# A two-layer block on one core: short-lived tiles share rings, the token and unit rings grow, and the order is drawn anew

## The chip, the cores and the metric

The kernel runs on one core of a Trainium2 chip. A core has five engines with a queue of their own each: TensorE (PE, matrix products; PEld is its loading of weights), VectorE (DVE), ScalarE (ACT), GpSimd (POOL) and SyncE (SP, which here only issues DMAs). Each engine works through its instructions in the order in which the program put them, and they meet through semaphores. The metric is the device time of one execution in microseconds. Before the change it is 3841.9 us, the median of three executions (3837.64 to 3845.13).

## The reference, cut to what matters

The input x is 32 images of 56 x 56 positions (tokens) with 128 channels. Two layers follow each other, and in each of them a "conv" part and an "ffn" part is added to x.

```python
x = x + L0_conv(ln_c(x))      # batch norm over all tokens, signs, a 3x3 convolution with signs as weights
t = t + L0_ffn(ln_t(t))       # softmax over 8 experts, the best 2 per token, each expert a 128x128 matrix
x = x + L1_conv(ln_c(x))      # per image and per 16 channels: a = sigmoid(p1*p2), b likewise,
                              #   z = einsum('bikc,bkjc->bijc', a, b); gate * (ln(z) @ Wz + bz)
t = t + L1_ffn(ln_t(t))       # 64 experts; each takes its best 8 tokens of every image, pools them,
                              #   two layers with gelu, and adds its output to those 8 tokens
```

The batch norm needs the mean and the variance of all 32 images before the first convolution can be compared with its limit. The product z of L1_conv needs a whole image, and so does the choice of 8 tokens of L1_ffn.

## The kernel before

**Tiling.** A unit is 896 tokens, seven rows of 128 with 128 channels: 3584 bytes in each partition. Two images make a pair of seven units; there are 16 pairs and 112 units.

**Stages.** A first pass (`fetch1`, `stats1`, `norm1`) reads all units, normalises them, turns them by TensorE, stores them and gathers the batch norm's sums. `load_weights` prepares weights meanwhile. `batch_norm` closes it. Then each pair goes through these stages: `fetch` loads a unit's x, `sign` compares the stored values with the limit, `conv` and `conv_back` do the convolution and add it; `moe_stats`, `moe_turn`, `moe_route`, `moe_gates` choose two of eight experts for each token, `moe_experts` multiplies (VectorE scales the turned tokens by the gates in L823, TensorE does eight products in L828), `moe_add` adds. `tri_stats` and `tri_turn` prepare the product of L1_conv. Then comes a chain with little width, called the triangle below: `tri_b` and `tri_a` each make two products per half (L886), ScalarE writes them to `lines` (L899), TensorE turns those (`tr_b`, `tr_a`, by the helper at L473), ScalarE and VectorE multiply the two parts (L914, L919), ScalarE takes the sigmoids (L933 for b, L945 for a); `tri_z` does the product (L972), normalises, and takes z through DRAM into `zc` (L1051). `tri_out` uses it unit by unit and adds to x. `gate_stats`, `gate_turn`, `gate_logits`, `top8` (the best 8 of 3136 tokens on VectorE, and an exponential over all of them on ScalarE, L1211 and L1214) and `pool_rows` do the pair's part of L1_ffn. At the end `late_experts` runs the 64 experts in 16 groups of four for all pairs at once, six groups a second time for the last pair alone, and GpSimd adds their outputs to the tokens in DRAM by 128 indirect DMAs (L1497), two chains of 64 in which each waits until the one before it has landed. `last_sums` and `last_out_rows` finish the last pair.

**What sets the order.** No engine's order is written by hand. Every operation is put into the class `Order` with its engine, an assumed duration in ns, and what it reads and writes. Its rank is a tick: `p * PERIOD + TICK[stage][i]`, with a period of 14 ticks a pair (L1917 to L1923). `Order.run` (L164) then plays the work through in the kernel's own build: at each moment each free engine takes the ready operation of lowest rank whose tiles can be had, for as long as the assumed duration says. The order in which operations are taken is the order in which they are written into the engines' queues. The chip then runs this order with its own durations. Assumed durations and ticks thus change nothing of what is computed, only what stands behind what in each queue.

**Tiles and rings.** A tile is taken from a ring of equal buffers named by a tag (L426 to L431). Before: 12 token tiles "x" and 5 unit tiles "u" of 3584 bytes, 4 "xT" and 3 "yl" of that size, 5 "gb" of 4096 bytes for gates, and small rings of their own for tiles that live briefly: "st1", "q1", "rm1" in the first pass, "rT" in `moe_route`, "abm" (2), "b", "zT" in the triangle, "pt" in `pool_rows`. A pair holds seven "x" tiles from `fetch` to the store in `gate_turn` (L1131). The late experts take "x" tiles too, five a group (L1330, L1379).

Of the kernel before, what the change touches and what calls it, by code (L numbers as in the profile page):

```python
# [25 lines left out]
H = 56  # L26
# [12 lines left out]
    "fetch": (1.14, 2.61, 2.37, -0.16, 7.91, 9.69, 13.32),  # L39
    "sign": (0.38, 0.8, 0.81, 5.7, 6.62, 8.09, 11.62),  # L40
    "conv": (2.4, 3.69, 6.8, 7.72, 10.43, 11.89, 12.86),
    "conv_back": (2.88, 4.08, 7.34, 7.86, 10.43, 11.92, 14.91),
    "moe_turn": (4.53, 5.17, 9.52, 8.55, 12.68, 12.47, 15.14),
    "moe_gates": (6.43, 7.52, 9.89, 10.15, 13.98, 12.85, 16.56),
    "moe_experts": (7.18, 7.67, 10.31, 10.83, 14.93, 12.94, 16.8),
    "moe_add0": (10.78, 13.85, 13.48, 12.98, 18.39, 17.9, 18.29),
    "moe_add1": (10.06, 12.78, 13.45, 11.14, 15.45, 13.84, 17.8),
    "tri_turn": (15.73, 17.37, 18.31, 18.26, 19.34, 19.61, 19.71),
    "moe_stats": (4.26, 8.17, 12.25, 14.94),
    "moe_route": (5.48, 9.71, 12.84, 15.88),  # L50
    "tri_stats": (14.82, 13.52, 18.41, 19.02),
    "tri_b": (19.79, 19.99),
    "tri_a": (19.82, 21.57),
    "tri_z": (21.72,),
    "tri_out": (22.38, 23.42, 24.57, 25.03, 26.33, 28.33, 30.18),
    "gate_stats": (23.97, 24.69, 27.63, 30.31),
    "gate_turn": (25.8, 26.15, 26.94, 28.19, 29.43, 32.04, 32.1),
    "gate_logits": (25.91, 27.01, 28.84, 29.87, 31.66, 33.33, 32.83, 33.54),
    "clear": (31.73,),
    "top8": (34.46,),  # L60
    "pool_rows": (37.33,),
    "late_first": (37.82, 37.92, 38.25, 41.79, 42.31, 42.85),
    "late_alone": (51.08, 41.11, 38.24, 41.73, 42.93, 41.08),
    "late_rest": (39.41, 40.01, 40.1, 40.59, 42.76, 44.26, 47.21, 48.79, 50.74, 58.57),
    "last_sums": (49.02,),
    "last_rows": (63.85,),
# [4 lines left out]
NX, NY = 12, 5  # L71
# [212 lines left out]
def kernel(ctx: ExitStack, tc: tile.TileContext, a: dict, out: bass.AP):  # L284
# [118 lines left out]
    with ExitStack() as c2:  # L403
# [19 lines left out]
        for t in lines:  # L423
# [3 lines left out]
            "x": NX, "u": NY, "ps": 8, "gb": 5, "xT": 4, "yl": 3, "st1": 2, "q1": 2, "rm1": 2,  # L427
# [256 lines left out]
        def moe_route(p, m):  # L684
# [82 lines left out]
            @op("ACT", 210, r=[d], w=[(d, 1)])  # L767
            def _():
                nc.scalar.activation(d.ap[:, 1, :], d.ap[:, 0, :], AF.Sigmoid)
                nc.scalar.activation(d.ap[:, 2, :], d.ap[:, 0, :], AF.Sigmoid, scale=-1.0)  # L770
# [1252 lines left out]
```

## Time and profile before

| | us |
|---|---|
| median of three executions | 3841.9 (3837.64 to 3845.13) |
| the profiled execution | 3851.35 |
| its span, first to last instruction | 3849.5 |
| TensorE busy in the span | 3495.7 |
| VectorE busy | 3149.1 |
| ScalarE busy | 2355.4 |
| GpSimd busy | 407.0 |
| mean granted clock of TensorE | 0.958 |
| from the first pair's product z (L972) to the last pair's, 15 periods | 548.49 to 3476.28 |

The profile gives for each engine its busy time, for each line its instructions and mean duration, and for each idle stretch what ended it ("<-"). The chain of work that ended last goes back from the last instruction to whatever released each step. A table by stretch gives, for windows of the span, each engine's busy time and count of instructions, and TensorE's granted clock (1.00 is full speed). Products in f32 show as two records each. The execution has three parts: the first pass up to about 345 us, the pairs with one period after the other up to about 3500 us, and the additions to the tokens from 3501.23 to 3844.7 us.

### The profile page before, as it was taken

Reading aid. Unit: us, or ns where it says so; the run is one execution under the profiler, and the core shown is the slowest. Engines: PE = TensorE matmul, PEld = TensorE weight load, DVE = VectorE, ACT = ScalarE, POOL = GpSimd, SP = SyncE. Lnnn points to the kernel's source line nnn. Section 1 sums busy time; section 2 is a strip of 40 time slices with the busy share of each in tenths; the row PEclk is TensorE's granted clock in tenths of the full one; section 3 lists DMA queues with packets and bytes.
Section 4 is the critical chain, followed back from the end, with each engine's and each line's share of the span. In section 5 each row is a group of like instructions: output and inputs, shape, how many; then the busy total and the mean of one; then the engine's idle time right before and its main releaser. Section 6 shows DMA issues by size and latency. Waiting matters only on the chain.

```text
span 3849.5 us, 77967 instructions
## 1 busy us (share of the span) xinstructions
PE 3495.7 (91%) x27661; PEld 2836.7 (74%) x27661; DVE 3149.1 (82%) x10452; ACT 2355.4 (61%) x5458; POOL 407.0 (11%) x472
## 2 busy tenths in 40 slices
PE   7999999999999999999999999999999999997653
PEld 6886787777777777778787868686878787865442
DVE  7997879898989898989898989898989898875310
ACT  5997437566666666675757575757575747566210
POOL 1000000100000000000000000101010101003667
PEclk9999999999999999999999999999999999998776
DMA  7997556465656565656565656565656565656774
GB/s 252 349 342 257 199 176 243 174 235 183 230 183 229 176 225 186 224 190 220 191 224 188 219 182 223 188 230 189 230 189 218 201 217 203 203 195 187 211 199 73
DMA packets 325544, 811.90 MB, mean 211 GB/s; under 512 B 86170, under 2 KB 110659, under 8 KB 325155
## 3 DMA queue, kind: packets, MB, share of 16 engines
q1 hardware_dynamic: 262034, 680.39, 51.4%
q10 hardware_dynamic: 41104, 109.20, 7.3%
q0 software_dynamic: 22016, 17.32, 3.1%
q8 instruction: 220, 3.60, 0.4%
q14 instruction: 170, 1.38, 0.1%
HBM read 630.19 MB, written 176.55 MB: 210 GB/s over the span
## 4 chain that ended last, share of the span: by engine, by line
PE 39%; DVE 33%; ACT 11%; DMA 9%; issue 4%; POOL 3%; ACTq 0%; another core or an unknown queue 0%; SPq 0%; DVEq 0%; POOLq 0%
PE acc L828 22%; DVE stln L484 8%; DVE gb L823 7%; DMA gb<-gate 4%; DVE sg L1098 3%; PE ps_cv L629 3%; DMA out<-eo_False,picked 3%; PE gram L1673 3%; POOL out L1497 2%; PE tr L473 2%; DVE x L1107 2%; DVE x L571 2%; ACT ym L558 1%; ACT yt L558 1%; PE ps_z L972 1%
## 5 line engine op out<-in xcount | busy, mean ns | idle before, releaser
L828 PE MATMUL acc<-expert_w,gb 128*128 128x128 f32 x12544 | 1443.9, 276 | 25.2 <-DVE gb L823 13.5
L828 PEld LDWEIGHTS acc<-expert_w,gb 128*128 128x128 f32 x12544 | 1415.1, 192 | 67.3 <-DVE gb L823 33.9
L823 DVE TENSOR_TENSOR gb<-gb,xT 128x1024 f32<-128x1024 f32 x784 | 949.4, 1217 | 64.5 <-DMA gb<-gate 61.5
L484 DVE BATCH_NORM_STATS2 stln<-x 128x6 f32<-128x128 f32 x2352 | 576.4, 281 | 1.9
L558 ACT ACTIVATE ym<-x,rmln 128x128 f32<-128x128 f32 x784 | 322.4, 486 | 244.4 <-DVE rmln L546 243.6
L629 PE MATMUL ps_cv<-frame,w_sign 128*128 128x448 bf16 x2016 | 427.5, 362 | 8.4 <-DVE frame L607 8.4
L558 ACT ACTIVATE yt<-x,rmln 128x128 f32<-128x128 f32 x784 | 324.5, 486 | 123.2 <-DVE rmln L546 120.0
L558 ACT ACTIVATE yl<-x,rmln 128x128 f32<-128x128 f32 x784 | 318.6, 487 | 125.9 <-DVE rmln L543 113.3
L629 PEld LDWEIGHTS <-w_sign 128*128 128x128 bf16 x2016 | 196.4, 99 | 188.5 <-issue 23.8
L1229 POOL DMA_INDIRECT rows<-y,near x128 | 122.2, 955 | 1113.5 <-DVE mk L730 1007.0
L1114 POOL MEMSET a_bd<- 128x2048 f32 x16 | 29.5, 1841 | 1846.3 <-PE ps_zo L1085 1400.7
L840 DVE TENSOR_TENSOR x<-acc,x 128x512 f32<-128x512 f32 x224 | 137.9, 616 | 95.7 <-PE acc L828 95.6
L1497 POOL DMA_INDIRECT out<-eo_False,picked x128 | 197.1, 1540 | 139.0 <-DMA out<-eo_False,picked 74.8
L558 ACT ACTIVATE y<-x,rm 128x128 f32<-128x128 f32 x448 | 194.7, 486 | 20.2 <-DVE rm L543 11.3
L637 ACT ACTIVATE cv<-ps_cv,cv_shift,cv_scale 128x448 f32<-128x448 f32 x224 | 157.9, 725 | 74.8 <-PE ps_cv L629 74.3
L1063 PEld LDWEIGHTS ps_g<-wg,yT 128*128 128x128 f32 x1568 | 187.7, 193 | 21.6 <-issue 15.1
L1063 PE MATMUL ps_g<-wg,yT 128*128 128x128 f32 x1568 | 203.5, 280 | 0.0
L484 DVE BATCH_NORM_STATS2 st<-x 128x6 f32<-128x128 f32 x784 | 179.6, 278 | 24.5 <-DMA x<-in_x 24.2
L1673 PE MATMUL gram<-y 128*128 128x128 f32 x1568 | 196.7, 278 | 0.0
L1673 PEld LDWEIGHTS gram<-y 128*128 128x128 f32 x1568 | 192.3, 198 | 0.0
L579 ACT COPY xT<-trm 128x512 f32<-128x512 f32 x224 | 108.6, 528 | 98.9 <-PE trm L473 79.4
L473 PE MATMUL tr<-ident,y 128*128 128x128 f32 x784 | 139.2, 295 | 29.1 <-ACT y L558 23.1
(244 smaller groups left out, 5295.0 us busy)
## 6 DMA issues: line engine op xcount, KB each, us to landing
gb<-gate SPq DMA_DIRECT2D x784, 512.0 KB
x<-in_x SPq DMA_DIRECT2D x224, 448.0 KB
y<-yT SPq DMA_DIRECT2D x112, 448.0 KB
ys<-y SPq DMA_DIRECT2D x112, 448.0 KB
out<-x ACTq DMA_DIRECT2D x112, 448.0 KB
y<-yl ACTq DMA_DIRECT2D x112, 448.0 KB
w_False<-in_L_ffn_weight SPq DMA_DIRECT2D x128, 256.0 KB
w_True<-in_L_ffn_weight SPq DMA_DIRECT2D x48, 256.0 KB
```

The source lines that it names most:

```text
L473: nc.tensor.transpose(ps.ap[:, n * 128 : (n + 1) * 128], get()[:, n0 + n, :], ident)
L484: nc.vector.bn_stats(st.ap[:, c0 + k, :], src.ap[:, k, :])
L558: nc.scalar.activation(dst.ap[:, k, :], src.ap[:, k, :], AF.Identity, bias=m, scale=r)
L629: nc.tensor.matmul(acc, lhsT=w_sign[:, tap, :], rhs=frames[f][:, 8 * band + kh : 8 * band + kh + 8, kw : kw + W], start=(tap == 0), stop=( ...
L637: nc.scalar.activation(cv.ap[:, :, 64 * h : 64 * h + 64], ps.ap[:, :448].rearrange("c (q n) -> c n q", n=N7), AF.Identity, bias=cv_shift, ...
L823: nc.vector.tensor_tensor(gb.ap, gb.ap, over(xT.ap[:, n, :], E0), ALU.mult)
L828: nc.tensor.matmul(acc.ap[:, n % 4 * C : (n % 4 + 1) * C], lhsT=gb.ap[:, e, :], rhs=expert_w[:, e * C : (e + 1) * C], start=(e == 0), stop ...
L840: nc.vector.tensor_tensor(dst, acc.ap[:, : k * C], dst, ALU.add)
L1063: nc.tensor.matmul(psg.ap[:, n * C : (n + 1) * C], lhsT=yT[:, n0 + n, 16 * u : 16 * u + 16, :].rearrange("c r v -> c (r v)"), rhs=wg, star ...
L1229: nc.gpsimd.indirect_dma_start(out=rows.ap[:, j, :], out_offset=None, in_=y3_d[p], in_offset=bass.IndirectOffsetOnAxis(ap=near.ap[:, k + j ...
L1497: ins = nc.gpsimd.indirect_dma_start(out=tokens_out, out_offset=bass.IndirectOffsetOnAxis(ap=picked[lot][:rows, e : e + 1], axis=0), in_=e ...
L1673: nc.tensor.matmul(gram.ap[:, :C], lhsT=y.ap[:, n, :], rhs=y.ap[:, n, :], start=(g % G16 == 0 and n == 0), stop=(g % G16 == G16 - 1 and n ...
```

## The change

Ten rings of short-lived tiles go or shrink, and their tiles are taken from larger rings. In the first pass "st1" moves into "yl", and "q1" and "rm1" into "xT". "rT" moves into "u". "abm" (two buffers), "b" and "zT" move into "yl". "pt" moves into "pacc". "lg", "k1" and "k2" keep one buffer in place of two. This frees 16,960 bytes of each partition: 1344 + 448 + 448 (first pass), 2048 (rT), 3 x 448 (lg, k1, k2), 4096 (abm), 3584 (b), 3136 (zT), 512 (pt). Three more "x" and one more "u" tile take 14,336.

Six assumed durations on ScalarE are raised: the gates' sigmoids from 210 to 430 ns, those of b from 540 to 960 and 780, those of a from 1000 to 1800 (two instructions), each copy to `zc` from 750 to 1650, and the exponential of `top8` from 2700 to 4300.

All ticks are new. The instructions that are run, their number and their operands stay as they were, but for the buffers that they name.

```diff
 TICK = {
-    "fetch": (1.14, 2.61, 2.37, -0.16, 7.91, 9.69, 13.32),
+    "fetch": (-3.74, -10, -3.13, -14.5, -7.83, 3.11, 10.08),
...
-    "conv": (2.4, 3.69, 6.8, 7.72, 10.43, 11.89, 12.86),
+    "conv": (1.55, 3.6, 7.13, 8.23, 10.33, 11.24, 12.47),
...
-    "moe_experts": (7.18, 7.67, 10.31, 10.83, 14.93, 12.94, 16.8),
+    "moe_experts": (9.97, 8.74, 10.4, 10.31, 14.58, 13.75, 18.16),
...
-    "tri_b": (19.79, 19.99),
-    "tri_a": (19.82, 21.57),
-    "tri_z": (21.72,),
-    "tri_out": (22.38, 23.42, 24.57, 25.03, 26.33, 28.33, 30.18),
+    "tri_b": (19.94, 20.51),
+    "tri_a": (20.49, 22.18),
+    "tri_z": (22.21,),
+    "tri_out": (22.65, 22.27, 24.57, 24.46, 25.73, 26.61, 29.54),
...
-    "gate_logits": (25.91, 27.01, 28.84, 29.87, 31.66, 33.33, 32.83, 33.54),
-    "clear": (31.73,),
-    "top8": (34.46,),
-    "pool_rows": (37.33,),
-    "late_first": (37.82, 37.92, 38.25, 41.79, 42.31, 42.85),
-    "late_alone": (51.08, 41.11, 38.24, 41.73, 42.93, 41.08),
-    "late_rest": (39.41, 40.01, 40.1, 40.59, 42.76, 44.26, 47.21, 48.79, 50.74, 58.57),
-    "last_sums": (49.02,),
-    "last_rows": (63.85,),
+    "gate_logits": (25.65, 27.25, 29.32, 29.3, 30.74, 32.14, 33.59, 34.2),
+    "clear": (29.96,),
+    "top8": (34.73,),
+    "pool_rows": (37.11,),
+    "late_first": (37.25, 38.05, 39.03, 42.4, 43.15, 50.78),
+    "late_alone": (72, 45.56, 46.46, 53.51, 72.6, 48.13),
+    "late_rest": (39.44, 41.8, 46.7, 48.82, 51.44, 55.75, 55.79, 59.9, 61.33, 63.15),
+    "last_sums": (43.28,),
+    "last_rows": (77.43,),
 }
...
-NX, NY = 12, 5
+NX, NY = 15, 6
...
         op = Order({
-            "x": NX, "u": NY, "ps": 8, "gb": 5, "xT": 4, "yl": 3, "st1": 2, "q1": 2, "rm1": 2,
-            "st": 3, "q": 3, "rT": 1, "lg": 2, "k1": 2, "k2": 2, "mk": 2, "d": 2,
-            "gg": 2, "gT": 2, "rm": 4, "abm": 2, "b": 1, "zq": 1, "zT": 1, "lgT": 1,
-            "m8": 2, "i8": 2, "sq": 2, "pg": 2, "near": 2, "pacc": 1, "ptc": 1, "pt": 1,
+            "x": NX, "u": NY, "ps": 8, "gb": 5, "xT": 4, "yl": 3,
+            "st": 3, "q": 3, "lg": 1, "k1": 1, "k2": 1, "mk": 2, "d": 2,
+            "gg": 2, "gT": 2, "rm": 4, "zq": 1, "lgT": 1,
+            "m8": 2, "i8": 2, "sq": 2, "pg": 2, "near": 2, "pacc": 1, "ptc": 1,
         })
...
-            rT = new("rT", [128, 512], f"rT_{name}")
+            rT = new("u", [128, 512], f"rT_{name}")
...
-            @op("ACT", 210, r=[d], w=[(d, 1)])
+            @op("ACT", 430, r=[d], w=[(d, 1)])
...
-            u = new("abm", [128, NV, 4, CH], f"abm_{name}")
+            u = new("yl", [128, NV, 4, CH], f"abm_{name}")
...
-                live[p]["b"] = new("b", [128, CH, W], f"b_s_{p}")
+                live[p]["b"] = new("yl", [128, CH, W], f"b_s_{p}")
...
-            @op("ACT", 540, r=[(u, 0), (u, 4)], w=[(b_s, h)])
+            @op("ACT", (960, 780)[h], r=[(u, 0), (u, 4)], w=[(b_s, h)])
...
-            @op("ACT", 2 * 500, r=[(u, 0), (u, 4)], w=[("a_bd", h)])
+            @op("ACT", 2 * 900, r=[(u, 0), (u, 4)], w=[("a_bd", h)])
...
-            zT = new("zT", [128, N7, 2, H], f"zT_{p}")
+            zT = new("yl", [128, N7, 2, H], f"zT_{p}")
...
-                @op("ACT", 750, r=[(zv, rg) for rg in range(4)],
+                @op("ACT", 1650, r=[(zv, rg) for rg in range(4)],
...
-            @op("ACT", 2700, r=[q, m8], w=all_lg + [(q, 1), (pg, 1)])
+            @op("ACT", 4300, r=[q, m8], w=all_lg + [(q, 1), (pg, 1)])
...
-            pk = new("pt", [2 * K1, 2 * E1], f"pt_{p}")
+            pk = new("pacc", [2 * K1, 2 * E1], f"pk_{p}")
...
-            st = new("st1", [128, G4 * N7, 6], f"st1_{k}")
+            st = new("yl", [128, G4 * N7, 6], f"st1_{k}")
...
-            rm = first["rm", k] = new("rm1", [128, 2, G4 * N7], f"rm1_{k}")
+            rm = first["rm", k] = new("xT", [128, 2, G4 * N7], f"rm1_{k}")
...
-                0.0, "q1",
+                0.0, "xT",
```

More of the change, by code (lines that the diff above doesn't have):

```diff
@@ L38 @@
 TICK = {
-    "fetch": (1.14, 2.61, 2.37, -0.16, 7.91, 9.69, 13.32),
-    "sign": (0.38, 0.8, 0.81, 5.7, 6.62, 8.09, 11.62),
-    "conv": (2.4, 3.69, 6.8, 7.72, 10.43, 11.89, 12.86),
-    "conv_back": (2.88, 4.08, 7.34, 7.86, 10.43, 11.92, 14.91),
-    "moe_turn": (4.53, 5.17, 9.52, 8.55, 12.68, 12.47, 15.14),
-    "moe_gates": (6.43, 7.52, 9.89, 10.15, 13.98, 12.85, 16.56),
-    "moe_experts": (7.18, 7.67, 10.31, 10.83, 14.93, 12.94, 16.8),
-    "moe_add0": (10.78, 13.85, 13.48, 12.98, 18.39, 17.9, 18.29),
@@ L47 @@
[L47 to L51, printed above, removed]
-    "tri_b": (19.79, 19.99),
-    "tri_a": (19.82, 21.57),
-    "tri_z": (21.72,),
-    "tri_out": (22.38, 23.42, 24.57, 25.03, 26.33, 28.33, 30.18),
-    "gate_stats": (23.97, 24.69, 27.63, 30.31),
-    "gate_turn": (25.8, 26.15, 26.94, 28.19, 29.43, 32.04, 32.1),
@@ L58 @@
-    "gate_logits": (25.91, 27.01, 28.84, 29.87, 31.66, 33.33, 32.83, 33.54),
-    "clear": (31.73,),
-    "top8": (34.46,),
-    "pool_rows": (37.33,),
-    "late_first": (37.82, 37.92, 38.25, 41.79, 42.31, 42.85),
-    "late_alone": (51.08, 41.11, 38.24, 41.73, 42.93, 41.08),
-    "late_rest": (39.41, 40.01, 40.1, 40.59, 42.76, 44.26, 47.21, 48.79, 50.74, 58.57),
-    "last_sums": (49.02,),
-    "last_rows": (63.85,),
+    "fetch": (-3.74, -10, -3.13, -14.5, -7.83, 3.11, 10.08),
+    "sign": (-0.46, 0.58, 0.99, 5.76, 7.43, 9.35, 7.45),
@@ new lines @@
+    "conv": (1.55, 3.6, 7.13, 8.23, 10.33, 11.24, 12.47),
+    "conv_back": (3.49, 4.12, 7.45, 8.99, 10.33, 11.5, 14.37),
+    "moe_turn": (4.64, 5.02, 9.64, 9.61, 12.11, 12.05, 15.86),
+    "moe_gates": (7.34, 7.19, 9.81, 10.29, 13.07, 12.37, 17.81),
+    "moe_experts": (9.97, 8.74, 10.4, 10.31, 14.58, 13.75, 18.16),
+    "moe_add0": (12.93, 12.5, 11.9, 14.5, 16.21, 16.41, 18.99),
+    "moe_add1": (13.44, 10.15, 13.46, 11.4, 14.97, 14.28, 18.83),
+    "tri_turn": (17.2, 17.23, 18.18, 18.85, 18.85, 19.68, 19.73),
@@ new lines @@
+    "moe_stats": (4.59, 9.39, 11.74, 14.89),
+    "moe_route": (5.55, 9.69, 12.24, 16.09),
+    "tri_stats": (15.5, 14.58, 18.73, 19.51),
+    "tri_b": (19.94, 20.51),
+    "tri_a": (20.49, 22.18),
+    "tri_z": (22.21,),
+    "tri_out": (22.65, 22.27, 24.57, 24.46, 25.73, 26.61, 29.54),
+    "gate_stats": (23.28, 25.16, 26.82, 30.79),
+    "gate_turn": (24.56, 25.82, 26.81, 27.98, 30.07, 32.08, 31.98),
+    "gate_logits": (25.65, 27.25, 29.32, 29.3, 30.74, 32.14, 33.59, 34.2),
+    "clear": (29.96,),
```

## The prediction

> **What bounds the kernel now.** I read the page's busy times first. No engine is full over the span:
>
> ```profile
> PE 3495.7 (91%) x27661; PEld 2836.7 (74%) x27661; DVE 3149.1 (82%) x10452; ACT 2355.4 (61%) x5458; POOL 407.0 (11%) x472
> ```
>
> Such a share mixes stages, so next comes the table by stretch: thirteen whole periods, then the neighbourhood of one triangle in steps of 5 us (window: length, then busy us of PE, PEld, DVE, ACT, POOL, granted clock, DMA share, GB/s).
>
> ```profile
> 743.00:3286.00 2543.00, 2415.89 (x19650) 1972.11 (x19650) 2264.88 (x7133) 1632.28 (x3639) 142.67 (x130) 0.99 0.59 207
> 1105.00:1110.00 5.00, 5.00 (x37) 3.06 (x39) 4.86 (x15) 4.97 (x10) 1.90 (x2) 1.00 0.06 15
> 1110.00:1115.00 5.00, 2.76 (x34) 0.92 (x23) 3.25 (x17) 4.70 (x6) 3.78 (x4) 1.00 0.20 52
> 1115.00:1120.00 5.00, 2.99 (x20) 1.09 (x18) 3.76 (x6) 2.04 (x6) 3.50 (x3) 1.00 0.14 39
> 1120.00:1125.00 5.00, 4.07 (x20) 2.38 (x21) 2.60 (x9) 4.26 (x10) 0.00 (x0) 0.50 0.05 15
> 1125.00:1130.00 5.00, 5.00 (x36) 3.50 (x36) 2.69 (x9) 4.66 (x11) 0.00 (x0) 0.82 0.00 0
> ```
>
> A period is 2543 / 13 = 195.6 us. TensorE is busy 185.8 of it and VectorE 174.2, so TensorE bounds the period and idles 9.8. The rows show where: from 1110 to 1125 it misses 2.24 + 2.01 + 0.93 us, and then works at half clock. The clock costs 4.07 x 0.5 + 5 x 0.18 = 2.9 us. The waits of TensorE in the same thirteen periods agree (total us, times, longest):
>
> ```profile
> PE tr_a L473 <- ACT lines L899: 40.6, 24, 2.3
> PE tr_b L473 <- issue: 38.4, 13, 3.7
> PE acc L828 <- DVE gb L823: 12.1, 41, 0.8
> ```
>
> The first two are (40.6 + 38.4) / 13 = 6.1 us a period, both for the transposes of `lines`. With the clock the triangle loses 9.0 us in each period; all else together 3.7. ScalarE's instructions in time order say why `lines` is late:
>
> ```profile
> 1108.14 1.28 ACT L1211 ACT_TABLE_LOAD   x1
> 1109.44 0.30 ACT L1211 ACTIVATE pg<-m,sq 128x8 f32<-128x8 f32 x1
> 1109.64 2.90 ACT L1214 ACTIVATE lgT<-lgT,sq 128x3136 f32<-128x3136 f32 x1
> 1112.45 0.18 ACT L1214 ACTIVATION_READ_ACCUMULATOR lgT<-lgT,sq 128x1 f32 x1
> 1112.54 0.71 ACT L637 ACTIVATE cv<-ps_cv,cv_shift,cv_scale 128x448 f32<-128x448 f32 x1
> 1113.15 0.62 ACT L899 ACTIVATE lines<-ps_b,bb 128x448 f32<-128x448 f32 x1
> ```
>
> The exponential of `top8` holds ScalarE from 1108.14 to 1112.6, 4.5 us, where the plan assumes 2.7. The products for b were done by 1111; their copy to `lines` stands behind it, and TensorE's queue behind that copy. Groups by line give the other assumed durations:
>
> ```profile
> L945 ACT ACTIVATE a_bd<-abm_a 56x448 f32<-56x448 f32 x64 | 63.9, 999 | 19.8 <-DVE acc L1249 10.4 <-DVE abm_a L919 9.0
> L1051 ACT COPY a_bd<-zv 128x896 f32<-128x896 f32 x32 | 55.1, 1774 | 5.5 <-DMA zv<-z 5.5
> L933 ACT ACTIVATE b_s<-abm_b 128x512 f32<-128x512 f32 (+1 forms) x32 | 31.6, 988 | 0.0
> ```
>
> Against assumptions of 500, 750 and 540. In the end part the 128 additions bound the time: 343.5 us from 3501.2 to 3844.7, of which these waits are part:
>
> ```profile
> POOL out L1497 <- DMA out<-eo_False,picked: 74.8, 47, 4.6
> ```
>
> [...]
>
> **The change part by part.** *Assumed durations.* Between the products for b and the product z, per pair: the exponential was short by 4.5 - 2.7 = 1.8 us, b by 2 x 0.99 - 1.08 = 0.9, a by 4 x 1.0 - 2.0 = 2.0, together 4.7. The new figures cover 1.6 + 0.66 + 1.6 = 3.9 of it. The old plan so believed the triangle 4.7 us shorter than it is, and left about that much too little other work in TensorE's queue between its transposes; the chip shows 6.1 us idle. A plan that knows of 3.9 can put 3.9 us of convolutions, turns and experts there. I take the idle time as falling from 6.1 to 2.2, and [...] half of the clock's 2.9 comes back: 3.9 + 1.4 = 5.3 us. Work put there must be ready, and some will be missed elsewhere: I take 5.0 a period. VectorE then stands at 174.2 / 190.6 = 91%, still below TensorE. Over 15 periods: 75 us. The `zc` copies (short by 2.05) and the gates' sigmoids (0.84) lie beside experts' products (TensorE is at 5.00 of 5 us after 1135): nothing, and up to 0.5 us a period if that cover is thin.
>
> *Three more "x" tiles.* No instruction is added. SP's own waits in two periods show the ring in use:
>
> ```profile
> SPq L592 <- ACT yl L558: 57.7, 14, 11.6
> ```
>
> SP stands 29 us a period before x loads, with gate loads (L817) queued behind. Yet TensorE's wait through VectorE's gates is 12.1 / 13 = 0.9 us a period, since five "gb" buffers of 8 x 0.223 = 1.8 us each cover 9 us (the chain in order of time runs 448 records in 50.03 us, two to a product). So the ring alone is worth 0 to 0.9; its use is to give the triangle work from the next pair, which I counted above.
>
> *Tiles that move.* "yl": the last `ylT` is read at 1098.5, the first abm copy runs at 1119, z leaves at 1159, the next `ylT` is written at 1188: 20 and 29 us free on the two sides, cost 0. If they met, ScalarE's abm copy would stand before the last `ps_l`, with the copies to `lines` behind it and TensorE's transposes behind those, us for us. "u" holds `rT` for a copy and four transposes, 0.59 + 0.66 us, four times a pair, and has one buffer more: 0. "lg", "k1", "k2" with one buffer serialise batches that stand 60, 57 and 20 us apart (first copies near 1107, 1167, 1224, 1244); 0, or up to a batch's chain of 4 us if two come together. `pk` in "pacc" lives from 1129 to 1134.4, its ring is next wanted a period later: 0. First pass: "yl" and "xT" have no other user but `mean_w`.
>
> *First pass.* From 60 to 100 us, where the weights' four tiles sit in a ring of 5 "u", TensorE is busy 35.09 of 40 at clock 0.83: some 11 us lost. A sixth "u" doubles what is left for the units; I take 4. At the turn to the pairs (340 to 360: 11.62 of 20) earlier x loads may give 2. Bounds 0 and 15.
>
> *End.* The ticks of the late experts are reordered, with the same 128 additions. At best half of the 74.8 us of waits goes (-37); a worse interleaving of the two chains costs as much (+37). I take 0.
>
> Sum on the profiled execution: 3851.4 - 75 - 6 = 3770. It stands 9.4 above the median, so 3761 against 3841.9.
>
> **The rivals.** *The stall goes wholly* (chance 0.15): all 9.0 us x 15 = 135, and the first pass 6: 3701. For it: the expert products are plenty (392 x 0.223 = 88 us a pair). Against: the new ticks still put `tri_b` (19.94) and `tri_z` (22.21) before the next pair's first experts (8.74 + 14 = 22.74), so only ready convolutions, turns and leftover experts are there.
>
> *The change doesn't do what it says* (0.17): the stall is one of data, not of order; each transpose waits for its copy and the filler is not ready. Then only the first pass gains: 3836. For it: 6 us of the wait is "issue" and short pieces. Against: VectorE and ScalarE idle in it as well, so it is order, not load.
>
> *Slower: x loads at the head of SP's queue* (0.16). The new fetch ticks (-14.5 to 10.1) make SP take an x load as soon as the plan sees a buffer free, and the buffer comes free after a store and a normalisation on ScalarE that the chip may end later. SP waits in order, and gate loads stand behind. It decides once a wait outlasts the 9 us that the "gb" ring covers; the longest now is 12.1. Seven loads a pair, each 1.5 us beyond the cover, cost 10 us, less the gain of 5: +5 x 15 = 75, thus 3917.
>
> **How the numbers follow.** The likeliest case, a partly filled triangle, has 0.52 and 3761 (own range 3725 to 3805 with the end's bound). The range 3700 to 3850 leaves out about 0.07 below and 0.13 above. A measurement of this kernel tells 0.2%, some 8 us, from no change. Faster by more than that: 0.51 + 0.15 + 0.10 of the second rival = 0.76; within it 0.08; slower 0.16.
>
> **What would show it.** Right: the distance of z products falls from 195.2 to about 190; the two waits of TensorE for `lines` fall below 3 us a period and the clock's dip in the triangle shrinks; VectorE's waits for gates stay near 61.5 / 16 = 4 us a pair; the additions still take about 343 us. Wrong: the dip unchanged at an unchanged period, x loads at SP with longer waits followed by VectorE idling for gates, or a `tri_b` or `tr_b` waiting for a "yl" reader. The sum fails if the gain sits in the first pass or the end.

## The result, and the profile after

The changed kernel takes 3820.7 us (median of five executions, 3802.54 to 3828.05) against 3842.0 of the kernel before (median of five, 3837.64 to 3848.67). The ratio of the means is 0.9933, with a 95% interval of 0.9905 to 0.9961; all ratios below are of means too. The change makes the kernel faster, by 21 us where 81 were forecast.

The page of the changed kernel, busy time of each engine, and below it the table by stretch: first the same thirteen periods, then one triangle and what follows it (window: length, then busy us of PE, PEld, DVE, ACT, POOL, granted clock, DMA share, GB/s).

```profile
PE 3486.8 (91%) x27661; PEld 2840.6 (74%) x27661; DVE 3154.8 (83%) x10452; ACT 2359.6 (62%) x5456; POOL 409.4 (11%) x472
```

```profile
743.00:3286.00 2543.00, 2433.09 (x19753) 1993.44 (x19751) 2276.47 (x7152) 1643.78 (x3643) 145.09 (x130) 0.99 0.60 208
1290.00:1295.00 5.00, 5.00 (x48) 2.22 (x41) 2.59 (x8) 4.85 (x5) 2.00 (x3) 1.00 0.05 13
1295.00:1300.00 5.00, 3.09 (x29) 2.07 (x26) 3.05 (x10) 4.97 (x12) 3.87 (x4) 1.00 0.23 57
1300.00:1305.00 5.00, 3.33 (x23) 1.09 (x19) 4.72 (x19) 4.94 (x12) 3.50 (x3) 1.00 0.15 39
1305.00:1310.00 5.00, 4.44 (x30) 3.13 (x31) 2.81 (x11) 4.77 (x11) 0.00 (x0) 1.00 0.19 23
1320.00:1325.00 5.00, 5.00 (x33) 5.00 (x33) 5.00 (x8) 1.49 (x4) 0.00 (x0) 0.70 0.20 57
```

In the same 2543 us TensorE is busy 17.2 us more than before (2433.1 against 2415.9), 1.3 us a period. The triangle still has its hole: from 1295 to 1310 TensorE misses 1.91 + 1.67 + 0.56 = 4.1 us. In this period the half clock is no longer inside it but behind the product z, which starts at 1310.8 (the row 1320 to 1325). ScalarE is now full throughout the triangle (4.85, 4.97, 4.94, 4.77 of 5). TensorE's waits in the thirteen periods (total us, times, longest):

```profile
PE tr_a L473 <- ACT lines L899: 35.1, 26, 1.9
PE acc L828 <- DVE gb L823: 19.0, 31, 2.5
PE trm L473 <- ACT ym L558: 15.3, 39, 0.5
PE acc L828 <- DVE rmln L543: 9.5, 11, 0.9
PE tr_b L473 <- ACT lines L899: 1.4, 1, 1.4
```

The wait at `tr_b` is nearly gone (3.0 us a period before, 0.1 now), that at `tr_a` is 2.7 us where it was 3.1. The two together fell from 6.1 to 2.8. The rest of the list is new or larger: gates 0.9 to 1.5 us, `trm` 1.2, `rmln` 0.7. ScalarE in order of time shows what became of the exponential:

```profile
1289.97 1.39 ACT L899 ACTIVATE lines<-ps_b,bb 128x448 f32<-128x448 f32 x2 [0.19 <-PE ps_b L886]
1291.38 1.28 ACT L1211 ACT_TABLE_LOAD   x1
1292.67 0.30 ACT L1211 ACTIVATE pg<-m,sq 128x8 f32<-128x8 f32 x1
1292.88 2.89 ACT L1214 ACTIVATE lgT<-lgT,sq 128x3136 f32<-128x3136 f32 x1
1295.77 0.62 ACT L914 COPY abm_b<-tr_b 128x256 f32<-128x256 f32 x2
1296.29 1.07 ACT L899 ACTIVATE lines<-ps_a,ba 128x392 f32<-128x392 f32 x2
```

It was moved by one step. It now stands behind the copies of b to `lines` and ahead of those of a, so that `tr_a` waits where `tr_b` did. It did not leave the triangle. Two waits outside it, SP's before x loads in the thirteen periods and GpSimd's at the additions of the end:

```profile
SPq L592 <- ACT yl L558: 372.6, 78, 18.6
POOL out L1497 <- DMA out<-eo_False,picked: 80.9, 52, 4.6
```

SP stands before x loads as long as before in all (374.9 us in the same window there, 91 times), though the longest wait grew from 12.1 to 18.6 us. The additions bound the end as they did, 342.9 us (3471.28 to 3814.2) against 343.5.

Where the two profiled executions differ, from the trace of each (us, L972 is the product z):

| stretch | before | after | difference |
|---|---|---|---|
| start to the first pair's z | 548.3 | 533.7 | -14.6 |
| the next 14 periods, each | 195.6 | 194.8 | -0.8 (14: -11.4) |
| the last period | 190.0 | 187.6 | -2.4 |
| last z to the end | 373.2 | 371.0 | -2.2 |
| span | 3849.5 | 3818.9 | -30.6 |
| in each of the 14 periods: TensorE idle | 9.76 | 8.45 | -1.3 |
| ... lost to the half clock | 2.1 | 2.2 | +0.1 |

The profiled execution of before stood 9.4 us above its median and that of after at its median, which is why the spans differ by 30.6 and the medians by 21.4. In which rows these 9 us lie is not known, so the gains in the table may be too large by as much in all. The stretch before the first z alone varies between runs with the same first pass (544.4 to 550.2 in those below that keep it).

### The profile page after: what moved, and what is told of

Read it like the earlier page. It is cut to its first block, busy times and chain, and to the rows that moved or that the text cites. A ratio compares the mean times of both kernels' runs of the same rounds, so it can differ in the third digit from the quotient of the medians.

```text
span 3818.9 us, 78066 instructions
## 1 busy us (share of the span) xinstructions
PE 3486.8 (91%) x27661; PEld 2840.6 (74%) x27661; DVE 3154.8 (83%) x10452; ACT 2359.6 (62%) x5456; POOL 409.4 (11%) x472
## 4 chain that ended last, share of the span: by engine, by line
PE 52%; DVE 20%; DMA 14%; ACT 8%; POOL 3%; issue 3%; SPq 0%; ACTq 0%; POOLq 0%; DVEq 0%
PE acc L828 27%; DMA gb<-gate 9%; PE ps_cv L629 5%; PE gram L1673 4%; DMA out<-eo_False,picked 4%; DVE gb L823 4%; PE tr L473 3%; DVE stln L484 2%; POOL out L1497 2%; DVE sg L1098 2%; PE trm L473 2%; PE ps_g L1063 2%; PE ps_z L972 1%; PE trl L473 1%; PE trc L473 1%
## 5 line engine op out<-in xcount | busy, mean ns | idle before, releaser
L828 PE MATMUL acc<-expert_w,gb 128*128 128x128 f32 x12544 | 1488.1, 279 | 42.0 <-DVE gb L823 23.6
L828 PEld LDWEIGHTS acc<-expert_w,gb 128*128 128x128 f32 x12544 | 1447.0, 194 | 102.8 <-DVE gb L823 39.0
L484 DVE BATCH_NORM_STATS2 stln<-x 128x6 f32<-128x128 f32 x2352 | 564.5, 283 | 1.8
L558 ACT ACTIVATE yl<-x,rmln 128x128 f32<-128x128 f32 x784 | 335.3, 490 | 88.3 <-DVE rmln L543 80.6
L558 ACT ACTIVATE y<-x,rm 128x128 f32<-128x128 f32 x448 | 211.9, 724 | 22.7 <-DVE rm L543 15.9
L1063 PEld LDWEIGHTS ps_g<-wg,yT 128*128 128x128 f32 x1568 | 186.2, 192 | 30.5 <-DVE q_ln L540 11.7
L579 ACT COPY ylT<-trl 128x512 f32<-128x512 f32 x224 | 113.7, 531 | 130.5 <-PE trl L473 130.5
L840 DVE TENSOR_TENSOR x<-acc,x 128x512 f32<-128x512 f32 (+1 forms) x224 | 138.5, 618 | 47.0 <-PE acc L828 46.8
```

The lines of the kernel that those rows point to most:

```text
L484: nc.vector.bn_stats(st.ap[:, c0 + k, :], src.ap[:, k, :])
L558: nc.scalar.activation(dst.ap[:, k, :], src.ap[:, k, :], AF.Identity, bias=m, scale=r)
L579: nc.scalar.copy(t.ap[:, n0 : n0 + k, :].rearrange("c n p -> c (n p)"), ps.ap[:, : k * 128],)
L828: nc.tensor.matmul(acc.ap[:, n % 4 * C : (n % 4 + 1) * C], lhsT=gb.ap[:, e, :], rhs=expert_w[:, e * C : (e + 1) * C], start=(e == 0), stop ...
L840: nc.vector.tensor_tensor(dst, acc.ap[:, : k * C], dst, ALU.add)
L1063: nc.tensor.matmul(psg.ap[:, n * C : (n + 1) * C], lhsT=yT[:, n0 + n, 16 * u : 16 * u + 16, :].rearrange("c r v -> c (r v)"), rhs=wg, star ...
```

## The experiments

Each changes a copy of one of the two kernels. Line numbers in their profiles shift by a few where code was added. "Period" is the mean over the 14 distances of z products from the first on (195.6 before, 194.8 after); each profile is of one execution. A ratio is always to the kernel before as it was measured beside that experiment, where its median lay between 3844 and 3856 us. So ratios may be compared across experiments, and times only within one; a period carries the same doubt of some 0.3%, 0.6 us.

**The parts one by one.** The change has three: durations, rings, ticks. First the six durations alone, with everything else as before:

```diff
-            @op("ACT", 2700, r=[q, m8], w=all_lg + [(q, 1), (pg, 1)])
+            @op("ACT", 4300, r=[q, m8], w=all_lg + [(q, 1), (pg, 1)])
...
```

> The kernel before with the six longer ScalarE durations alone (old ticks, old rings). If the plan's wrong durations caused the stall at the lines copies: the waits of TensorE for tr_b and tr_a fall from 6.1 us a period to 3 or less, and most of the change's gain is here already, 0.993 to 0.996 of before. If the gain comes from the first pass and from ticks drawn for the new rings: 0.998 to 1.005, since the old ticks were drawn with the old durations.

Measured: 4094.2 us, 1.0642 (1.0624 to 1.0659). The period is 211.4 us. The waits of `tr_b` and `tr_a` did fall, from 6.1 to 3.9 us, as was hoped of true durations, but TensorE is idle 17.0 us a period and the clock costs 7.2.

Then the rings alone (15 token and 6 unit tiles, all moved tiles), with the old durations and ticks:

```diff
-NX, NY = 12, 5
+NX, NY = 15, 6
...
-            u = new("abm", [128, NV, 4, CH], f"abm_{name}")
+            u = new("yl", [128, NV, 4, CH], f"abm_{name}")
...
```

> The kernel before with the moved tiles, 15 token tiles and 6 unit tiles alone (old ticks, old durations). If the rings are worth nothing by themselves, as predicted (0 to 0.9 us a period, 4 to 6 us in the first pass): 0.997 to 1.000, with the waits for the lines copies unchanged at 6 us a period. If room was what the plan lacked: 0.990 to 0.995, the period shorter by 1 us or more.

Measured: 3894.3 us, 1.0123 (1.0105 to 1.0141), period 199.1. With more room to draw in, the order came out slower.

Then two of three: durations and ticks on the old rings, and rings and ticks with the old durations.

> New durations and new ticks on the old rings (12 token tiles, 5 unit tiles, small rings of their own). If the order alone makes the gain: 0.993 to 0.997, periods near 194.6 us. If the new ticks lean on the larger rings: slower than before, 1.002 to 1.02, with longer waits of SP before x loads and of VectorE for gates.

> New ticks and new rings with the old durations. If the durations matter: the wait for tr_b comes back (2 to 3 us a period) and the time goes back to 0.997 to 1.003 of before. If ticks and rings alone made the gain: 0.992 to 0.995.

Measured: 4212.8 us, 1.0958 (1.0938 to 1.0978), and 3988.0 us, 1.0362 (1.0345 to 1.0379). All four lie outside every range expected of them. What follows from them: the parts have no worth of their own that could be added. Each is a different input to the same drawing of the order, and ticks fit the durations and rings for which they were drawn. The change is one thing, a new order.

One thing can be told apart, the gain before the first z. It needs the new rings and the new ticks, and hardly the durations: the first z comes at 535.4 us with rings and ticks, at 542.7 with the rings alone, and at 545.9 with durations and ticks on the old rings (548.3 before, 533.7 after).

**Is the exponential the cause of the stall?** The exponential over all tokens is cut to 448 of 3136 at the same place in the same queues. This leaves most of the softmax's sum out; it takes 2.2 us from ScalarE in each pair (the exponential lasts 0.65 us in place of 2.89) and nothing else.

```diff
-                    lg.ap, lg.ap, AF.Exp, bias=q.ap[:, 0:1], accum_out=q.ap[:, 1:2]
+                    lg.ap[:, :448], lg.ap[:, :448], AF.Exp, bias=q.ap[:, 0:1], accum_out=q.ap[:, 1:2]
```

> The changed kernel, every instruction in the same place of its queue, but the exponential of top8 runs over 448 of 3136 tokens (its sum is that of 448 tokens, so the weights of the pooled tokens are other numbers); some 2.4 us less on ScalarE in each pair. If ScalarE's exponential in the triangle still sets TensorE's wait for tr_a: that wait falls from 2.7 us a period to below 1, the period from 194.6 to about 192.5, the time to 0.985 to 0.989 of before. If TensorE's own work and the other waits bound the period: under 0.5 us a period, 0.991 to 0.995.

> The kernel before with the same short exponential (448 of 3136 tokens summed), all queues unchanged. If the late exponential caused the stall at tr_b as the prediction said: the wait for tr_b falls from 2.9 us a period to below 1, the clock dips less often, the period falls by 2 to 3.5 us, 0.987 to 0.992. If the wait moves to the next transposes: less than 1 us a period, 0.996 to 1.000.

Measured: on the changed kernel 3794.6 us, 0.9866 (0.9847 to 0.9885), period 192.9; on the kernel before 3790.0 us, 0.9851 (0.9838 to 0.9864), period 191.4. TensorE's waits of the two, in the thirteen periods, the changed kernel first:

```profile
PE trg L793 <- DVE gg L779: 26.0, 12, 2.6
PE tr_a L473 <- ACT lines L899: 2.7, 4, 1.1
```

```profile
PE tr_a L473 <- ACT lines L899: 29.9, 13, 2.3
PE tr_b L473 <- ACT lines L899: 14.6, 13, 1.3
```

In the kernel before, 2.2 us less on ScalarE shorten the period by 4.2: the waits at `tr_b` and `tr_a` fall from 6.1 to 3.4, and the clock's loss from 2.1 to 0.7. So the late exponential does cause a good part of the stall, 2.7 of 6.1 us, and most of the dip; 3.4 us of waits stay, with some 2.2 us of table load, first exponential and short exponential still in the same place. In the changed kernel `tr_a` waits 0.2 us in place of 2.7, but only 1.9 us of the period go, since `trg` waits 2.0 in place of 0.6. And the two kernels come out level: with the exponential short, the new order's period is 1.5 us the longer one, and that eats what its first pass gains.

**Is the room worth something?** The kernel before with its own order, instruction for instruction, and 14 token tiles, for which abm and b go into "yl". The order is drawn with the old rings; only where a tile is made does it come from the new ones:

```diff
+REAL = {'yl': 3, 'x': 14, 'u': 5}
+REAL_TAG = (('abm_', 'yl'), ('b_s_', 'yl'))
...
+        tag = next((t for start, t in REAL_TAG if name.startswith(start)), tag)
+        bufs = REAL.get(tag, bufs)
```

> The order of the kernel before, operation for operation, but the tiles lie in 14 token tiles in place of 12, and abm and b in the ring yl: room without a new plan. As predicted, room alone is worth 0 to 0.9 us a period: 0.996 to 1.000, SP's waits before x loads (29 us a period) nearly gone. If those waits cost time: 0.990 to 0.995. If yl readers hold back the triangle: 1.003 or more.

Measured: 3833.8 us, 0.9969 (0.9959 to 0.998), period 194.8. SP's wait before x loads in the same window:

```profile
SPq L598 <- ACT yl L564: 140.4, 13, 11.8
```

That is 140 us in place of 375. The room is thus worth 0.3%, nearly half of the change's 0.67%, if the order does not change with it. (All of the new rings under the old order weren't tried.) But it is not shown that SP's queue brought it. TensorE's waits for gates are as before (12.9 us in the thirteen periods, 12.1 before); what changed are its waits in the triangle, here of this run:

```profile
PE tr_b L479 <- ACT lines L905: 39.7, 26, 1.8
PE ps_a L892 <- DVE abm_b L925: 17.5, 13, 1.5
PE tr_a L479 <- ACT lines L905: 15.1, 19, 2.3
```

The waits for `lines` fall from 6.1 to 4.2 us a period, and 1.3 come back before the second products for a. In the kernel before, ScalarE itself stands in the triangle: some 2 us a period before the copy of abm, for TensorE, and 1.0 us before b's second copy to `lines`, released by something that the profile does not name:

```profile
ACT abm_b L914 <- PE ps_b L886: 23.3, 10, 3.0
ACT lines L899 <- remote: 12.9, 13, 1.7
```

Neither wait is there in this run, nor in the one with the short exponential on the kernel before. In this run the exponential is as long as ever, so its length alone does not account for the stall. The token tiles and the place of abm and b changed together here, and which of them took these waits away was not tried.

**Can the exponential leave the triangle, with an order drawn for that?** It gets a stage and a tick of its own behind the squares of the next pair's z (in all pairs but the last two), and all ticks are searched anew from those of the change. Alongside: the old rings with the new durations, and the new rings with the old durations, each with ticks searched for just that combination.

```diff
-            @op("ACT", 4300, r=[q, m8], w=all_lg + [(q, 1), (pg, 1)])
+            then = [("zsq", p + 1)] if weighed_late(p) else []
+            @op("ACT", 4300, r=[q, m8] + then, w=all_lg + [(q, 1), (pg, 1)])
...
+    "weigh": (22.87,),
```

> The changed kernel with the exponential of top8 held back until the squares of the next pair's z have been read (so it stands behind the triangle on ScalarE), and the ticks searched anew for that. Theory (the exponential, moved by one step only, keeps the triangle's wait for lines at 2.7 us a period): tr_a's wait for lines falls below 1 us a period, the period from 194.8 to about 192, the time to 3780 to 3795, 0.983 to 0.988 of the kernel before. Rival (what leaves the triangle returns as waits elsewhere, as it did in the change itself): the period stays at 194 or more and the time within 0.3% of the changed kernel, 0.990 to 0.996.

> The kernel before with its own rings (12 token tiles, 5 unit tiles, every short-lived tile where it was), the six new durations of ScalarE, and ticks searched for just this combination. Theory (the order needs the room: with true durations the old rings leave fewer orders to choose from): slower than the kernel before, 3850 to 3900. Rival (the prediction's view: true durations and ticks drawn up for them fill the triangle, the rings are worth nothing by themselves): about the time of the changed kernel, 3810 to 3830.

> The changed kernel with its rings, the old durations of ScalarE in the plan, and ticks searched for just this combination. Theory (true durations matter: a plan that takes ScalarE for faster than it is runs later on the chip than it was drawn, in the triangle above all): tr_a and tr_b wait 5 us or more a period together, the time 3800 to 3840, no better than the changed kernel. Rival (room and a fresh search are all there is to it): below 3790, faster than the changed kernel.

Measured: 3860.7 us, 1.0017 (1.0007 to 1.0027); 3975.3 us, 1.0315 (1.03 to 1.033); 3857.8 us, 1.0005 (0.9994 to 1.0016). All three lie outside their ranges. The first is a plain miss of the theory; its rival had the period right (194 or more) and the time too low. Its trace has the exponential where it was wanted, behind z, under 12.7 us of expert products, and no wait at `tr_a`; yet the period is 197.4. TensorE's longest wait there, and ScalarE in order of time (L915 and L638 are the copies from `tr_b` and of `cv` in this kernel):

```profile
PE trc L474 <- ACT cv L638: 51.6, 26, 4.4
```

```profile
1309.22 1.99 ACT L946 ACTIVATE a_bd<-abm_a 56x448 f32<-56x448 f32 x2
1314.82 0.37 ACT L915 COPY abm_b<-tr_b 128x256 f32<-128x256 f32 x1 [3.61 <-PE ps_a L887]
...
1316.77 0.70 ACT L638 ACTIVATE cv<-ps_cv,cv_shift,cv_scale 128x448 f32<-128x448 f32 x1
```

The hole is there again, 4.0 us a period, with another cause: ScalarE stands 3.6 us before a copy from `tr_b`, a copy of `cv` is queued behind it, and TensorE's turn `trc` behind that. Why that copy waits until TensorE is through its products for a, the trace does not tell; it stays open, as with the like wait before the copy of abm in the kernel before. The other two say little on rings and durations, since how good a searched order is depends on the search. In the third, `tr_a` and `tr_b` wait under 2 us a period together where its theory had 5 or more.

**Place, or amount of work?** No order is drawn from here on; the plan stays as it is and single instructions change. First the exponential in four pieces of 784 tokens, with one (before) or two (after) of ScalarE's next instructions after each:

```diff
-                nc.scalar.activation(lg.ap, lg.ap, AF.Exp, ..., accum_out=q.ap[:, 1:2])
+                piece(0)
+                later.extend(lambda i=i: piece(i) for i in (1, 2, 3))
...
+                nc.vector.tensor_reduce(q.ap[:, 1:2], q.ap[:, 2:6], AX.X, ALU.add)
```

> The kernel before, nothing planned anew: the exponential of top8 is cut into four pieces of 784 tokens, and after each piece one of ScalarE's next instructions (a cv copy, the two copies to lines) goes ahead; the four sums are added on VectorE. Theory (what hurts is that 4.5 us stand in one block ahead of the copies that TensorE waits for): the copies to lines run 1.3 and 0.6 us earlier, ScalarE works some 0.6 us more in all, so tr_b's wait falls by about 1 us a period, the clock's loss with it, and the time by 10 to 30 us, 0.992 to 0.997. Rival (ScalarE's sum of work in the triangle is what counts, as the runs with the short exponential also cut it): no gain or a loss, 1.000 to 1.004.

> The changed kernel, nothing planned anew: the exponential in four pieces, with two of ScalarE's next instructions after each (both abm_b copies, both copies of a to lines, both copies of b to lines); the sums are added on VectorE. Theory (the block): the copies of a to lines run about 1.3 us earlier, tr_a's wait of 2.7 us a period falls to about 1.4, the time to 3800 to 3812, 0.989 to 0.992. Rival (the sum of work): 0.993 to 0.997, as the changed kernel or slower.

Measured: 3691.6 and 3698.6 us, 0.9576 and 0.9599, and neither can be read as a time of the whole. In both the last pair's operations that hang on its exponential are left out, 80 of the 128 additions (48 at that line in the trace) with what leads to them. The periods before the last can be read, and they are longer, 196.4 us on both kernels. In the kernel before:

```profile
PE tr_a L499 <- ACT lines L925: 46.0, 25, 3.5
PE acc L854 <- DVE gb L849: 19.6, 43, 2.0
PE tr_b L499 <- ACT lines L925: 12.2, 7, 1.7
PE tr_b L499 <- issue: 9.9, 5, 2.9
```

The copies of b to `lines` start 4.0 and 5.4 us after the table load in place of 5.0 and 6.7. The waits at `tr_b` and `tr_a` fall from 6.1 to 5.2 us, and other waits take it back. The rival's forecast came true: no gain from breaking the block. That its reason, the sum of ScalarE's work, is the right one is not shown: the pieces also cost ScalarE 0.8 us more, and what reads the exponential is put off until the last piece.

Next the whole exponential held back by twenty of ScalarE's operations, with all that hangs on it, in every pair but the last:

```diff
+            if ops[k][3].__name__ == "weigh8" and k != last:
+                held, left = [k], 20
+            elif held and set(held) & set(ops[k][4]):
+                held.append(k)
```

> The kernel before, nothing planned anew: in all pairs but the last the whole exponential goes to ScalarE twenty operations later than planned, between the copies of b's second half and those of a's second half; what hangs on it is held back with it. Theory (a long instruction costs what stands behind it, wherever in the triangle it is): tr_b's wait of 2.9 us is gone, but the last copies to lines come later and TensorE waits for them at the second tr_a or at z; the time lies between 3800 and 3860. Rival (only the place ahead of the first copies hurts): 3790 or less, as with the short exponential.

> The same hold of twenty operations on the changed kernel: the exponential goes between the last two copies of tr_a, just ahead of the last a_bd. Theory: tr_a's wait of 2.7 us a period is gone, and the product z waits instead for a_bd, up to 4.5 us a period less what TensorE has to do there (18 products of the convolution, some 4 us): 3800 to 3850. Rival (only the place ahead of the first copies hurts): 3795 or less.

Measured: 3992.5 us, 1.0366 (1.0348 to 1.0383), and 3990.5 us, 1.0347 (1.0317 to 1.0377). Both theories missed. TensorE's first waits of the kernel before so changed (`tr_p` turns the pooled rows, L1272 in the kernel before):

```profile
PE tr_p L1290 <- DVE acc L1267: 103.6, 12, 10.8
PE tr_a L491 <- ACT lines L917: 47.6, 12, 4.8
```

The exponential has a reader in the triangle. VectorE weights the pooled rows with its result, and TensorE turns the sum, in order between `trc` and the second `tr_a`. Held back, it makes TensorE stand some 8 us a period for it. It can leave only together with `pool_rows`, as it did in the run with the exponential behind z.

Last, work leaves ScalarE and none is left out. The copies of abm and the copies of the blocked half to `lines` (b's first half before, a's first half after) run on VectorE at their planned places, and the reciprocal that waits for the exponential is held for three operations of ScalarE (six on the changed kernel), so that VectorE's queue does not stop for it ahead of them:

```diff
-                    nc.scalar.copy(u.ap[:, n0 : n0 + k], part(1))
+                    nc.vector.tensor_copy(u.ap[:, n0 : n0 + k], part(1))
...
-                    nc.scalar.activation(to, of, AF.Identity, bias=bias[:rows])
+                    if (x, h) == ("b", 0):
+                        nc.vector.tensor_scalar(to, of, bias[:rows], None, ALU.add)
+                    else:
+                        nc.scalar.activation(to, of, AF.Identity, bias=bias[:rows])
```

> The changed kernel, nothing planned anew and nothing left out: the abm copies, and the copies of a's first half to lines, run on VectorE in place of ScalarE, at their places in the plan; the reciprocal that waits for the exponential is held until six of ScalarE's later operations have been given out. Some 2.5 + 1.1 us a pair leave ScalarE in the triangle, and the copies to lines no longer stand behind the exponential. Theory (the triangle is bound by ScalarE's in-order queue): tr_a's wait of 2.7 us falls below 1, VectorE goes from 173 to about 176 us a period, the period to 190 to 193, the time to 3760 to 3800, 0.979 to 0.989. Rival (waits only move, VectorE's small chains now stand behind copies that wait for TensorE): period 194 or more, 0.992 to 1.01.

> The same on the kernel before: the abm copies and the copies of b's first half to lines on VectorE, the reciprocal held for three of ScalarE's operations. Theory: tr_b's wait of 2.9 us falls to below 1, tr_a's 3.2 to about 2, with some of the clock: the period from 195.2 to 189 to 192, the time 3760 to 3800, 0.977 to 0.987. Rival (waits only move): 0.997 to 1.01.

Measured: on the changed kernel 3807.8 us, 0.99 (0.9881 to 0.992), period 194.1; on the kernel before 3794.2 us, 0.9871 (0.9854 to 0.9887), period 191.8. On the changed kernel the waits for `lines` fall from 2.8 to 1.9 us a period, and `trg` takes 0.8 of it back: little comes of it. The second beats both kernels. Its thirteen periods, its waits in the triangle, and the two engines in order of time (L919 and L921 are the copies to `lines`, L936 those of abm):

```profile
743.00:3286.00 2543.00, 2447.20 (x20084) 2011.50 (x20082) 2353.21 (x7412) 1611.93 (x3558) 148.05 (x130) 0.99 0.60 210
```

```profile
PE tr_b L492 <- ACT lines L921: 25.5, 13, 2.0
PE tr_b L492 <- DVE lines L919: 13.9, 13, 1.1
PE tr_a L492 <- ACT lines L921: 4.7, 4, 1.2
```

```profile
1291.45 1.28 ACT L1233 ACT_TABLE_LOAD   x1
1292.96 2.90 ACT L1236 ACTIVATE lgT<-lgT,sq 128x3136 f32<-128x3136 f32 x1
1298.09 1.05 ACT L921 ACTIVATE lines<-ps_a,ba 128x392 f32<-128x392 f32 x2
```

```profile
1294.89 0.68 DVE L919 TENSOR_SCALAR lines<-ps_b,bb 128x448 f32<-128x448 f32 x1
1296.15 0.67 DVE L919 TENSOR_SCALAR lines<-ps_b,bb 128x448 f32<-128x448 f32 x1
1300.12 0.78 DVE L936 COPY abm_b<-tr_b 128x256 f32<-128x256 f32 x2
```

In the kernel before, the same part of a period reads:

```profile
1303.18 1.28 ACT L1211 ACT_TABLE_LOAD   x1
1314.37 0.65 ACT L914 COPY abm_b<-tr_b 128x256 f32<-128x256 f32 x2 [2.27 <-PE ps_b L886]
1314.91 1.08 ACT L899 ACTIVATE lines<-ps_a,ba 128x392 f32<-128x392 f32 x2
```

b's copies now run beside the exponential. a's copies follow 6.6 us after the table load. In the kernel before they came 11.7 us after it, in part because b's copies stood ahead of them and ScalarE stood 2.3 us for an abm copy. The waits at `tr_b` and `tr_a` are 3.4 us a period in place of 6.1, and the clock's loss 1.1 in place of 2.1. The size came as the theory had it, the place did not: `tr_b` still waits 3.0 us, and `tr_a` fell to 0.4. VectorE is no faster at these f32 tiles (0.67 to 0.68 us against 0.62 to 0.63 on ScalarE for a copy of 128x448), it only isn't behind the exponential.

Which of the two moves it was, and whether the room adds to it, was asked last: abm alone, and both moves with the 14 token tiles of the seventh run.

> As the run before (VectorE in place of ScalarE, on the kernel before), but only the abm copies move; the copies to lines stay on ScalarE behind the exponential. Theory (the amount of ScalarE's work in the triangle): most of the gain stays, 0.988 to 0.993. Rival (the place of the copies to lines behind the exponential): tr_b's wait stays near 2.9 us a period and the time at 0.995 to 1.0.

> The kernel before in its own order, with the copies of abm and of b's first half to lines on VectorE, and with the room of the seventh run (14 token tiles, abm and b in the ring of yl). Theory (the gains are of two different waits, SP's for token tiles and TensorE's for lines, so they add): 0.9871 - 0.003 = 0.984, 3785. Rival (the room is worth nothing once the triangle is short): 0.987.

Measured: 3836.8 us, 0.9978 (0.997 to 0.9986), period 194.6; and 3787.1 us, 0.9859 (0.9838 to 0.988), period 191.5. With abm alone TensorE waits for `lines` as long as ever:

```profile
PE tr_b L492 <- ACT lines L918: 76.7, 26, 4.1
```

That is 5.9 us a period, now all at `tr_b`. So it is b's copies behind the exponential that cost, and moving them on top brings 2.7 of the 3.8 us a period. That takes 1.2 us of work off ScalarE as well; but abm's copies took 2.5 us off it (0.65 + 0.61 + 0.65 + 0.57 in the kernel before) and brought 1.0, which speaks for the place and not the amount. b's copies alone, without abm, were not run. The last run has the lowest median of all kernels of the case that leave nothing out. Whether the room adds to it is not settled: the interval holds both the sum (0.984) and no addition (0.987).

## Why the prediction was right or wrong

*Direction and bound: right; cause: right in part.* TensorE bounds the period, its full-speed work hardly differs between the kernels (195.57 - 9.76 - 2.09 = 183.7 us a period, and 184.1 after), and the stall sat in the triangle behind the exponential; the runs with the short exponential show this for 2.7 of the 6.1 us. "Slower by x loads at the head of SP's queue" did not come, but its path is there: SP's waits are as long as before in all, the longest is 18.6 us against the 9 us of cover, VectorE waits longer for gates (85.0 us in the thirteen periods against 38.1), and TensorE pays 0.5 us a period of it.

*The step that failed* is the working of the 5.0 us a period, and two of its terms. Its first part, 3.9 us of filled idle time, nearly held: the two waits at the triangle fell by 3.3. As forecast, more work stands in it, nine products of the convolution and seven turns `trc` (2.3 us a period in all); the rest of the 3.3 is put down to the exponential's move behind b's copies.

The term "some will be missed elsewhere", put at 5.3 - 5.0 = 0.3 us, was mis-sized: all other idle time of TensorE grew from 3.7 to 5.65 us, by 2.0. The waits that grew (`acc` for gates and statistics, `trm`, `trg`) speak for ready work being scarce, so that what fills the triangle is missed where it covered something else; the prediction counted it as nearly free because expert products are plenty. That the filler itself is what is missed there is argued, not shown.

The other term, 1.4 us of clock, did not come at all. That half of the loss would come back with the shorter wait was the author's estimate; no trace showed it. It was also drawn too large: 2.9 us is the loss of the one triangle shown, the mean over fourteen periods is 2.1. From the first z to the fifteenth, the clock of either kernel stands at half for eighteen stretches of 3.41 us. Before, all lie in the triangle, starting 4 to 20 us ahead of z. After, six start there (12 to 13 us ahead), ten 8 to 10 us behind z, and two elsewhere; the loss is 2.2. Behind z is also where the whole new wait at `trm` lies, three short gaps a period.

So there is 3.3 - 2.0 = 1.3 us less idle time, of which the period shows 0.8; the rest is the 0.1 of clock and 0.4 of busy time, whose ends the profile models. Against 75 us predicted for fifteen periods the profiles give 11.4 + 2.4 = 14. So about half of the gain sits in the first pass, which the prediction had named as a sign that its sum fails.

*What lay behind it.* The prediction took the raised durations for knowledge that an order can turn into filled time. The new order did fill some, and it put the exponential one step later in the same triangle, where its result is wanted by `tr_p`, a reader that the prediction did not follow; taken out together with that reader, behind z, it brought no gain either. Nor were the durations worth anything by themselves: alone they cost 6.4%.

*First pass and turn*: predicted -6 with bounds 0 and 15, measured -14.6 in the two profiles, about -12 against the middle (546) of the runs with the old first pass. Under-sized, within the bounds. Whether the sixth unit tile did it, as predicted, was not tried alone.

*The ring alone*: predicted 0 to 0.9 us a period; at the unchanged order it brought 0.8 (195.6 to 194.8), 0.3% of the time. The size is right, at the upper end, by luck: the path named for it, SP's loads and TensorE's wait for gates, shows no gain, and the waits in the triangle do.

*Moved tiles at 0 and the end at 0*: no wait for a "yl", "u" or "pacc" buffer stands among the waits of the changed kernel's TensorE, and the additions take 342.9 us against 343.5. Right for this order. Under the old ticks the same rings cost 1.2%, which the argument by lifetimes did not see. Rings decide what the plan takes next and not only what must wait; that this is the reason is likely, since 14 token tiles under the unchanged order cost nothing, but not shown.

*The rivals*: the result lies between the likeliest case and "nothing but the first pass" (3836), nearer to the second. The range 3700 to 3850 held it.

## What to carry to other kernels

Where an order is drawn by a planner, a change of durations, rings or ranks is not a sum of parts but a new order, and taking a stall out of one place must be charged with what the filler covered before; here 2.0 of 3.3 us came back. Look for a long instruction that stands ahead of short copies in the same queue (here 2.9 us ahead of copies of 0.6), follow who reads its result before moving it, and first try to move the short copies to another engine: with copies of abm moved as well, that took 1.3% at the old plan where the new plan took 0.7%. A loss read from one sample period is to be checked against the mean before it is multiplied.

## What the runs showed of the hardware that was not expected

One stretch at half clock began with no long gap of TensorE before it. In the changed kernel the granted clock is 0.50 from 1319.63 to 1323.04. In the 3.41 us before, TensorE was busy 2.21 us in short pieces, its longest gap 0.54 us. A stretch just as busy in the same period (2.24 us, longest gap 1.18), shown first, was followed by full clock (1.00):

```profile
1299.15:1302.57 3.42, 2.24 (x22) 0.60 (x20) 2.54 (x10) 3.41 (x9) 2.81 (x4) 1.00 0.24 58
1302.57:1305.98 3.41, 2.36 (x17) 1.21 (x14) 2.24 (x10) 3.35 (x7) 1.32 (x1) 1.00 0.07 19
1316.22:1319.63 3.41, 2.21 (x9) 1.09 (x9) 3.41 (x5) 3.41 (x9) 0.00 (x0) 1.00 0.76 306
1319.63:1323.04 3.41, 3.41 (x18) 3.41 (x18) 3.41 (x5) 1.86 (x5) 0.00 (x0) 0.50 0.02 5
```

In the triangle that the prediction shows, the 3.41 us before the half clock (1116.57 to 1119.98) were busy 1.42 us. In the changed kernel the busy time of the stretch before, 2.21 and 2.24 us, does not tell the two cases apart. The stretch at 1316.22 held almost nothing but turns, the one at 1299.15 also 16 records of products for a; whether that decides stays open. The price here falls on what comes next, not on the gap: at half clock 18 records of TensorE fell into 3.41 us that were busy throughout, and 32 into the 3.41 us behind them, as busy and at full clock.

The pieces of the exponential with copies to `lines` between them needed no further table load in the trace (of the kernel before, 1306.67 to 1312.1), while the sigmoids behind them did (1.28 us). A piece of 784 columns with the reading of its sum held the queue for 0.93 us, four of them 3.7 in place of 2.9 for the whole: that is the price of cutting.
